# Layer 0's experts on one Trainium2 core: spreading routed vectors through DRAM in place of PE turns

## The chip, the core and the metric

The kernel runs on one core of a Trainium2 chip, as one launch. The metric is device time in microseconds (us), taken from the median of several runs; one further execution was recorded by the hardware profiler, and every profile line comes from that one. Engines are named as the profile names them: PE (matmuls, and turns by matmul with an identity), DVE, ACT and POOL (elementwise work), SP (which here only issues DMAs). ACT and POOL issue DMAs too.

## The reference, cut to what matters

Four layers follow each other; each adds a cross attention and a feed-forward part to `x` (4 sequences of 256 tokens, 256 wide, float32). The change lies in layer 0. Its feed-forward part routes every token to the 4 of 64 experts whose 16 projected values have the largest norm, sums the projections of the four, and sends the sum through all four's output matrices:

```python
x = x + _L0_xattn_ref(_layernorm(x), ctx, ...)      # 16 heads of width 16
x = x + _L0_ffn_ref(_layernorm(x), A, B, W, bias)

def _L0_ffn_ref(x, A, B, W, bias):                  # A: 64 x 16 x 256, B: 64 x 256 x 16
    vecs = jnp.einsum('arh,bsh->bsar', A, x)
    arrows = jnp.linalg.norm(vecs, axis=-1)
    _, idx = jax.lax.top_k(arrows, 4)
    routes = jax.nn.one_hot(idx, 64).sum(-2) / 4
    v = jnp.einsum('bsa,bsar->bsr', routes, vecs)
    delta = jnp.einsum('bsa,ajr,bsr->bsj', routes, B, v)
    return jnp.einsum('bsh,jh->bsj', x, W) + bias + delta
```

## The kernel before, in words

Tokens are worked in tiles of 128, two per sequence, so there are 8 tiles (n = 0 to 7; sequence n // 2). Everything named here is in `bounded_path`, in a block in which the code's order is the order on PE, ACT, DVE and POOL: nothing reorders instructions between the lines. SP takes its DMAs in code order as well.

**Opening** (lines 1057 to 1200, 1541 to 1600). DMAs bring the first sequence, the first context, the query, key and value weights and three rows of biases (`crow`, lines 1081 to 1086). The biases and weights are centred per head on DVE (`head_sums`, `centred`, lines 1173 to 1182). Three small matmuls spread the bias rows over 128 partitions (`spread_biases`, line 1188), with selecting rows `takes` that POOL makes (`rows_of_biases`, line 1120). `warm(n)` (line 1464) runs n matmuls of the identity that nothing reads.

**Layer 0's attention.** For each sequence b, eight half steps i (four head groups, two halves each) hold the scores of a head group on PE, their exponentials on ACT, and the values of the head group before. `between(b, i)` (line 1613) puts other work behind each half step: the next sequence's projections, the output of the sequence before, and in the last sequence the start of the experts. `quotient` (line 1428) divides a head group's values by its sums on DVE.

**Layer 0's experts.** `Arrows(n)` (line 1471) has a tile's steps:
- `vectors` (line 1479): four matmuls give 1024 projections per token; ACT copies and squares them into the two halves of the tile `two`.
- `routes` (line 1496): DVE sums the squares per expert, finds the four largest (lines 1502 to 1509), multiplies the projections by the 0 or 1/4 of their expert (line 1511) and sums over experts to the 16-vector `v` (line 1513). POOL then writes the product of route and `v`, 128 x 1024, over the squares (line 1514).
- `turned` (line 1516): PE turns this product in eight 128 x 128 pieces, ACT copies them to `uT`.
- `output` (line 1527): two pairs of matmuls (`ww`) and eight matmuls with `uT` (line 1535) accumulate the result; DVE adds the bias (line 1537), POOL adds it to `x` (line 1538).

The loop at line 1749 runs the tiles so that the routing of tile n + 2 comes before the turns and output of tile n. Between them it puts two kinds of other work: `layernorm_T` (line 939), which turns a sequence's normalized rows by four PE turns, and `next(fold)`: `folding` (line 1003) multiplies layer 1's raw attention weights into each other, 8 half folds, each with a group of matmuls whose results ACT and DVE copy. `load_raw` (line 987) brings these raw weights by SP's queue, four DMAs for each of four groups, with two groups' buffers.

Other parts of the kernel already turn rows without PE: `layernorm_aside` (line 969) turns 32 x 32 blocks on DVE and puts them in place by 16 DMAs on SP.

Of the kernel before, what the change touches and what calls it, by code (L numbers as in the profile page):

```python
# [9 lines left out]
F32 = mybir.dt.float32  # L10
# [826 lines left out]
def bounded_path(ctx: ExitStack, tc: tile.TileContext, t, out: bass.AP, over):  # L837
# [34 lines left out]
    def load_c(b):  # L872
        (nc.sync if b else nc.scalar).dma_start(c_sb[:, b], t["ctx"][b].rearrange("(k p) c -> p k c", p=P))
# [113 lines left out]
    def load_raw(L, i, after=None, tiles=None):  # L987

        wq, wk, wv, wo = (t[f"L{L}_{n}"] for n in ("wqT", "wkT", "wvT", "wo"))
        h0, g0 = 4 * i, 2 * i  # L990
        if tiles is None:
            tiles = [
                rawp.tile(shape, F32, tag=f"{n}_t", name=f"{n}_{L}_{i}")
                for n, shape in (("wq", [P, 4, D]), ("wk", [P, 2, DC]), ("wv", [P, 2, DC]), ("wo", [P, 4, D]))
            ]
        wq_t, wk_t, wv_t, wo_t = tiles
        for dst, src, a, z in ((wq_t, wq, h0, 4), (wk_t, wk, g0, 2), (wv_t, wv, g0, 2), (wo_t, wo, h0, 4)):
            dma = (nc.gpsimd if L == 2 else nc.sync).dma_start(dst, src[a * P : (a + z) * P, :].rearrange("(h e) d -> e h d", e=P))
            if after and L != 2:
                behind(dma, after)  # L1000
        raws[L, i] = wq_t, wk_t, wv_t, wo_t
# [53 lines left out]
    with tc.manual_schedule(engines={E.PE, E.Activation, E.DVE, E.Pool}):  # L1055
        c0 = ExitStack()
        l0 = c0.enter_context(tc.tile_pool(name="l0", bufs=1, side="right"))

        load_x(0)
        load_c(0)  # L1060
# [3 lines left out]
        wkv = l0.tile([P, 2, 2 * D], F32, tag="wkv", name="wkv")  # L1064
        nc.scalar.dma_start(wkv[:, 0, :], t["L0_wkv"])
# [5 lines left out]
        def by_head(w, x=HD0):  # L1071
            return w.rearrange("p n (h x) -> p n h x", x=x)


        rows1 = w0.tile([3, D + 3 * P], F32, tag="oT0", name="rows1")
        crow = rows1[:, :D].rearrange("n (o d) -> n o d", o=1)
        takes = rows1[:, D:].rearrange("n (i p) -> n i p", p=P)


        brow = l0.tile([1, 2, 2 * D], F32, tag="brow", name="brow")  # L1080
        nc.sync.dma_start(crow[0:1, 0, :], t["L0_bq"].partition_broadcast(1))
        for i, n in enumerate(("L0_bkv", "L0_bdca")):
            nc.sync.dma_start(
                crow[1 + i : 2 + i, 0, :].rearrange("o (h x) -> o h x", x=HD0),
                t[n].rearrange("(o h x) -> o h x", o=1, x=2 * HD0)[:, :, :HD0],
            )
# [16 lines left out]
        wb = load_fw("wb", [P, 8, D], lambda w: [(w, t["F0_bT"].rearrange("(k p) n -> p k n", p=P))], "wb", f0w)  # L1103
# [16 lines left out]
        def rows_of_biases():  # L1120
            nc.gpsimd.memset(takes, 1.0)
            for i, base, cm, p in (
                (0, 0, -1, 0), (1, -1, 1, 0), (1, 1, -1, 0), (2, RD - 1 - P, P, -1), (2, 2 * P - RD, -P, 1),
            ):
                nc.gpsimd.affine_select(
                    out=takes[:, i, :], in_=takes[:, i, :], compare_op=ALU.is_ge, fill=0.0, base=base,
                    pattern=[[p, P]], channel_multiplier=cm,
                )

        c_last = l0.tile([P, 2, 2, P], F32, tag="c_last", name="c_last")  # L1130
        nc.gpsimd.memset(c_last, 0.0)
# [56 lines left out]
        def spread_biases():  # L1188
            pb = bank("mm", [P, 2, D], "pbias0")
            for i in range(2):  # L1190
                nc.tensor.matmul(pb[:, i, :], lhsT=takes[:, i, :], rhs=crow[:, 0, :], start=True, stop=True)
            pl = bank("mm", [P, D], "pbias1")
            nc.tensor.matmul(pl, lhsT=takes[:, 2, :], rhs=crow[:, 0, :], start=True, stop=True)
            nc.scalar.copy(bqk[:, 0:2, :], pb)
            nc.scalar.copy(bqk[:, 2, :], pl)
# [111 lines left out]
        def columns_of_norms():  # L1307
# [5 lines left out]
            for o in range(2):  # L1313
                nc.vector.tensor_scalar(
                    cols[:, o, :], pairs[:, 0, :], halves0[:, o : o + 1], HD0 ** -0.5, ALU.mult, ALU.mult
                )
            nc.vector.tensor_copy(cols[:, 2:, :], pairs[:, 1:, :])
# [152 lines left out]

        class Arrows:
# [24 lines left out]
            def routes(self):  # L1496
# [11 lines left out]
                route = small.tile([P, NA], F32, tag="route", name=f"route{u}")  # L1508
                nc.vector.tensor_scalar(route, rest[:, :NA], 0.0, 1.0 / TOPA, ALU.is_lt, ALU.mult)
                route_b = route[:, :, None].to_broadcast([P, NA, RA])  # L1510
                nc.vector.tensor_tensor(ar, ar, route_b, ALU.mult)
                v = small.tile([P, RA], F32, tag="v", name=f"v{u}")
                nc.vector.tensor_reduce(v, ar.rearrange("p a r -> p r a"), AX.X, ALU.add)
                nc.gpsimd.tensor_tensor(sq, route_b, v[:, None, :].to_broadcast([P, NA, RA]), ALU.mult)

            def turned(self):
                self.uT = w0.tile([P, 8, P], F32, tag="qT0", name=f"uT{self.u}")
                for n in range(2):
                    pt = bank("t", [P, 4, P], f"puT{self.u}_{n}")
                    for k in range(4):  # L1520
                        a0 = 8 * (4 * n + k)
                        nc.tensor.transpose(
                            pt[:, k, :], self.two[:, 1, a0 : a0 + 8, :].rearrange("p a r -> p (a r)"), ident
                        )
                    nc.scalar.copy(self.uT[:, 4 * n : 4 * n + 4, :], pt)
# [15 lines left out]
        warm(9)  # L1541
        context_T(0)
        norm = Norm(0, "a0_0")
        rows_of_biases()
        last_context(0)
        mq = head_sums(by_head(wq0))
        xn = norm.tokens()
        warm(3)
        xnTs[0] = layernorm_T(xn, "a0_0")
        centred(by_head(wq0), by_head(wq0), mq)  # L1550
        centred(by_head(crow), by_head(crow), head_sums(by_head(crow), 3), 3)
# [6 lines left out]
        columns_of_norms()  # L1558
        warm(3)
        add_q = project_q(0)  # L1560
        spread_biases()
        add_q()
# [49 lines left out]

        def between(b, i):

            n = b + 1
            if n == 1:
# [76 lines left out]
            if b == B - 1:  # L1693
                if i in (0, 2, 6):
                    norms["f", i // 2] = Norm(min(i // 2, 2), f"f0_{min(i // 2, 2)}")
                if i in (1, 3, 7):
                    xns["f", i // 2] = norms["f", i // 2].tokens()
                if i in (3, 5):
                    k = (i - 3) // 2
                    xnTs["f", k] = layernorm_T(xns["f", k], f"f0_{k}")  # L1700
                if i == 4:
                    arrows[0] = Arrows(0)
                    arrows[0].vectors()
                if i == 5:
                    arrows[0].routes()
# [25 lines left out]
        arrows[1].routes()  # L1731
        arrows[0].turned()
        arrows[0].output()
        output0(B - 1)
# [14 lines left out]
        for n in range(B * NC):  # L1749
            if n + 2 < B * NC:  # L1750
                arrows[n + 2].routes()
            if n:
                arrows[n].turned()
            if n % NC == 0:
                if n + 3 < B * NC:
                    arrows[n + 3] = Arrows(n + 3)
                    arrows[n + 3].vectors()
                for _ in range((0, 0, 1, 1, 2, 2, 1, 1)[n]):
                    next(fold)
                if n == 6:  # L1760
                    xn1 = norm.tokens()
                if n:
                    arrows[n].output()
            else:
                k = n // NC + 2
                if k < B:
                    xnTs["f", k] = layernorm_T(xns["f", k + (k == 2)], f"f0_{k}")
                if n == 7:
                    first_xnT = layernorm_T(xn1, "a1_0")
                    next(fold)  # L1770
                arrows[n].output()
                for _ in range((0, 0, 1, 1, 2, 2, 1, 0)[n]):
                    next(fold)
                if n + 3 < B * NC:
                    arrows[n + 3] = Arrows(n + 3)
                    arrows[n + 3].vectors()
            if n == 5:
                norm = Norm(0, "a1_0")
            if n == 0:
                norm = Norm(3, "f0_3")  # L1780
            if n == 1:
                xns["f", 3] = norm.tokens()
            if 2 <= n < 2 + B:

                b = n - 2
                c2 = w0.tile([P, NK, DC], F32, tag="z0", name=f"c2_{b}")
                for k in range(NK):
                    nc.scalar.activation(
                        c2[:, k], c_sb[:, b, k], AF.Square, accum_out=csq[:, b * NK + k : b * NK + k + 1]
                    )  # L1790
# [1689 lines left out]
```

## Time and profile before

| what | value |
|---|---|
| median of 3 runs | 1381.64 us (1380.35 to 1382.58) |
| profiled execution | 1380.97 us, of it the span from first to last instruction 1379.2 us |
| PE busy in the span | 1369.2 us, 99% |
| DVE, POOL, ACT busy | 897.2, 699.4, 572.6 us |
| opening, to the first scores | 0 to 20.96 us |
| layer 0's attention | 20.96 to 137.39 us |
| layer 0's experts with layer 1's folds | 137.39 to 220.30 us, PE busy 82.91 us of it |
| DVE, ACT, POOL busy in the experts' stage | 58.06, 41.08, 26.09 us |
| the rest (layers 1 to 3) | 220.30 to 1379.2 us, PE busy 1150.95 us |

How to read its lines: a timeline line gives the start and the length in us, the engine, the line of the kernel, the operation, written tile<-read tiles, the shape and how many instructions are merged in it; in brackets the idle time of the engine ahead of it and what ended it. A matmul is recorded twice, in two halves, except a turn, which is one record; the end of a matmul reaches some 0.16 us into the next one. A window line gives the window, its length, the busy time of PE, weight loads, DVE, ACT and POOL with their counts, PE's granted clock as a share of full speed, the DMA engines' share and GB/s.

### The profile page before, as it was taken

Reading aid. Unit: us, or ns where it says so; the run is one execution under the profiler, and the core shown is the slowest. Engines: PE = TensorE matmul, PEld = TensorE weight load, DVE = VectorE, ACT = ScalarE, POOL = GpSimd, SP = SyncE. Lnnn points to the kernel's source line nnn. Section 1 sums busy time; section 2 is a strip of 40 time slices with the busy share of each in tenths; the row PEclk is TensorE's granted clock in tenths of the full one; section 3 lists DMA queues with packets and bytes.
Section 4 is the critical chain, followed back from the end, with each engine's and each line's share of the span. In section 5 each row is a group of like instructions: output and inputs, shape, how many; then the busy total and the mean of one; then the engine's idle time right before and its main releaser. Section 6 shows DMA issues by size and latency. Waiting matters only on the chain.

```text
span 1379.2 us, 20227 instructions
## 1 busy us (share of the span) xinstructions
PE 1369.2 (99%) x7221; PEld 903.1 (65%) x7221; DVE 897.2 (65%) x2052; ACT 572.6 (42%) x1134; POOL 699.4 (51%) x848
## 2 busy tenths in 40 slices
PE   9999999999999999999999999999999999999997
PEld 7665676566656667887565666666975665666666
DVE  6767863666666557655676756558656758566675
ACT  5766454433343332256434333333364334333331
POOL 5223333566565445352577655566325676444660
PEclk9999999999999999999999999999999999999999
DMA  5000220300000001361120000000432000000001
GB/s 171 15 3 2 77 78 17 89 19 8 16 5 19 0 13 43 83 218 48 47 54 15 17 0 16 0 1 16 124 119 69 7 12 4 1 8 1 0 1 34
DMA packets 77907, 50.79 MB, mean 37 GB/s; under 512 B 40628, under 2 KB 72645, under 8 KB 77799
## 3 DMA queue, kind: packets, MB, share of 16 engines
q1 hardware_dynamic: 72262, 36.13, 9.6%
q0 software_dynamic: 4176, 12.24, 3.1%
q8 instruction: 59, 0.97, 0.3%
q10 hardware_dynamic: 1360, 1.05, 0.2%
q14 instruction: 50, 0.40, 0.1%
HBM read 38.78 MB, written 6.95 MB: 33 GB/s over the span
## 4 chain that ended last, share of the span: by engine, by line
PE 97%; POOL 2%; DVE 1%; issue 0%; ACT 0%; POOLq 0%; DVEq 0%
PE ps L1948 23%; PE po L1956 23%; PE paq L1918 6%; PE pao L1918 5%; PE pbq L1918 4%; PE pbo L1918 4%; PE ps L1401 3%; PE po L1411 2%; PE pyf L1535 2%; PE paf L1485 2%; PE pgu L2496 2%; PE pm L1014 2%; PE psh L2317 2%; PE py L2042 2%; PE pn L1030 1%; PE pb L2901 1%
## 5 line engine op out<-in xcount | busy, mean ns | idle before, releaser
L1967 POOL TENSOR_TENSOR half<-pT 128x1024 f32<-128x1024 f32 x93 | 218.4, 2349 | 282.8 <-ACT pT L1951 228.0
L1948 PE MATMUL ps<-qT,cT 128*128 128x512 f32 x768 | 345.6, 593 | 0.0
L1956 PE MATMUL po<-pT,c_sb 128*128 128x512 f32 x768 | 345.3, 592 | 0.0
L1951 ACT ACTIVATE pT<-ps,mbias 128x512 f32<-128x512 f32 x384 | 263.8, 687 | 164.0 <-PE ps L1948 147.3
L1956 PEld LDWEIGHTS po<-pT,c_sb 128*128 128x128 f32 x768 | 145.8, 190 | 183.2 <-issue 183.2
L1948 PEld LDWEIGHTS ps<-qT,cT 128*128 128x128 f32 x768 | 138.9, 190 | 138.4 <-issue 136.1
L1960 ACT COPY oT<-po 128x512 f32<-128x512 f32 x96 | 56.2, 586 | 265.2 <-PE po L1956 265.2
L2003 POOL TENSOR_TENSOR oT<-oT,wide 128x512 f32<-128x512 f32 x84 | 106.8, 1291 | 0.0
L1928 DVE TENSOR_TENSOR qT<-qT,paq 128x128 f32<-128x128 f32 x90 | 25.2, 280 | 87.1 <-ACT qT L1927 87.1
L1405 ACT ACTIVATE pT<-ps 128x512 f32<-128x512 f32 x128 | 66.0, 602 | 21.6 <-PE ps L1401 21.4
L1975 DVE TENSOR_TENSOR half<-half 128x512 f32<-128x512 f32 x96 | 71.9, 749 | 2.7 <-POOL half L1965 2.5
L1977 DVE STREAM_TRANSPOSE turned<-half 128x512 f32<-128x512 f32 x96 | 68.3, 711 | 6.3
L1918 PE MATMUL paq<-xnT_a,m_sb 128*128 128x128 f32 x360 | 71.3, 280 | 0.0
L1928 DVE TENSOR_TENSOR w<-w,pao 128x128 f32<-128x128 f32 x21 | 6.0, 285 | 99.2 <-ACT w L1927 99.2
L1918 PE MATMUL paq<-xx,m_x 128*128 128x128 f32 x360 | 69.6, 275 | 0.0
L1918 PEld LDWEIGHTS paq<-xnT_a,m_sb 128*128 128x128 f32 x360 | 57.5, 192 | 18.2 <-issue 9.2
L1981 DVE TENSOR_REDUCE sums<-turned 128x16 f32<-128x512 f32 x96 | 65.9, 686 | 3.3
L1918 PE MATMUL pao<-n_x,ox 128*128 128x128 f32 x336 | 65.0, 275 | 0.0
L1927 ACT COPY qT<-paq 128x128 f32<-128x128 f32 x90 | 23.9, 265 | 94.2 <-PE paq L1918 93.2
L1931 DVE TENSOR_TENSOR qT<-qT,pbq 128x384 f32<-128x384 f32 x90 | 49.8, 554 | 9.4
L1918 PEld LDWEIGHTS paq<-xx,m_x 128*128 128x128 f32 x360 | 54.7, 192 | 0.0
L2002 DVE STREAM_TRANSPOSE wide<-rz 128x512 f32<-128x512 f32 x84 | 54.4, 686 | 0.0
(504 smaller groups left out, 2553.9 us busy)
## 6 DMA issues: line engine op xcount, KB each, us to landing
wq<-in_L_wqT SPq DMA_DIRECT2D x8, 512.0 KB
wo<-in_L_wo SPq DMA_DIRECT2D x8, 512.0 KB
yd<-yr SPq DMA_DIRECT2D x20, 128.0 KB
xnT_a<-y_a SPq DMA_DIRECT2D x144, 16.0 KB
xd<-xn_f SPq DMA_DIRECT2D x8, 256.0 KB
w<-in_F_w SPq DMA_DIRECT2D x4, 512.0 KB
wq<-in_L_wqT POOLq DMA_DIRECT2D x3, 512.0 KB
wo<-in_L_wo POOLq DMA_DIRECT2D x3, 512.0 KB
```

The lines of the kernel that those rows point to most:

```text
L1405: nc.scalar.activation(pT[kp][:, j], ps[j], AF.Exp)
L1918: nc.tensor.matmul(p[:, at, :], lhsT=lhsT, rhs=rhs, start=(k == 0 and at == 0), stop=(k == len(of) - 1 and i == which[-1]),)
L1948: nc.tensor.matmul(ps, lhsT=cT[:, b, k * P : (k + 1) * P], rhs=qT, start=True, stop=True)
L1951: nc.scalar.activation(pT[:, k, :], ps, AF.Exp, bias=mbias[:, b, k : k + 1])
L1956: nc.tensor.matmul(po, lhsT=c_sb[:, b, k, :], rhs=pT[:, k], start=(k == 0), stop=(k == NK - 1))
L1960: done["head"] = nc.scalar.copy(raw, po).ins
L1967: nc.gpsimd.tensor_tensor(half, pT[:, 0:2], pT[:, 2:4], ALU.add)
L1975: nc.vector.tensor_tensor(part, half[:, 0], half[:, 1], ALU.add)
L1977: nc.vector.transpose(turned.rearrange("p f i -> p (f i)"), part)
L1981: nc.vector.tensor_reduce(sums[b, hp // 4][:, hp % 4, :], turned, AX.X, ALU.add)
L2002: nc.vector.transpose(wide, rzs[b, hp // 4][:, hp % 4, :, None].to_broadcast([P, NB, 32]))
L2003: eng.tensor_tensor(outs[b, hp], outs[b, hp], wide.rearrange("p f i -> p (f i)"), ALU.mult)
```

## The change

1. **Turns.** Of a tile only two 128-wide pieces are turned on PE: the routes (written twice side by side, so that the turn has them on 128 partitions) and the 16-vector `v`. ACT copies both. The turned `v` (16 rows of 512 bytes) is written to a DRAM scratch by ACT's queue; SP then reads it back with two DMAs, each of which gives 64 partitions the same 4 KB (8 rows of `v`). POOL multiplies what has landed by the turned routes (`spread`), and the result takes the place of `uT`. The rows of `wb` are loaded in an order that fits.
2. **Order.** The loop over tiles is written out by hand, with `spread` of a tile just ahead of its `output`, and with other distances between `routes`, `turned` and `output`.
3. **Raw weights.** Layer 1's raw weights are loaded by POOL's queue: groups 0 and 1 behind the spread of tile 1, group 2 behind that of tile 4, group 3 behind that of tile 5.
4. **Expert rows.** For sequences 0 to 2 the normalized rows of the experts are turned by `layernorm_aside`, from the third sequence of layer 0's attention on; sequence 3 keeps its PE turns. Tile 0's vectors, routing, turns and spread move to earlier half steps of the last sequence.
5. **Opening.** The bias rows are loaded first, by ACT's queue, ahead of the context and of the key and value weights. `takes` is copied from the identity by DVE. The bias rows are centred and spread ahead of the queries; 11 warm matmuls at the start take the place of 9 and two times 3.

```diff
-            dma = (nc.gpsimd if L == 2 else nc.sync).dma_start(dst, src[...])
+            dma = (nc.gpsimd if L < 3 else nc.sync).dma_start(dst, src[...])
...
-                route = small.tile([P, NA], F32, tag="route", name=f"route{u}")
-                nc.vector.tensor_scalar(route, rest[:, :NA], 0.0, 1.0 / TOPA, ALU.is_lt, ALU.mult)
...
-                nc.gpsimd.tensor_tensor(sq, route_b, v[:, None, :].to_broadcast([P, NA, RA]), ALU.mult)
+                self.route = sq.rearrange("p a r -> p (a r)")[:, : 2 * NA].rearrange("p (h a) -> p h a", h=2)
+                nc.vector.tensor_scalar(
+                    self.route, rest[:, None, :NA].to_broadcast([P, 2, NA]), 0.0, 1.0 / TOPA, ALU.is_lt, ALU.mult
+                )
...
             def turned(self):
-                for n in range(2):
-                    pt = bank("t", [P, 4, P], f"puT{self.u}_{n}")
-                    for k in range(4):
-                        nc.tensor.transpose(pt[:, k, :], self.two[:, 1, a0 : a0 + 8, :]..., ident)
-                    nc.scalar.copy(self.uT[:, 4 * n : 4 * n + 4, :], pt)
+                pt = bank("t", [P, 2, P], f"prT{self.u}")
+                nc.tensor.transpose(pt[:RA, 1, :], self.v, ident)
+                nc.tensor.transpose(pt[:, 0, :], self.route.rearrange("p h a -> p (h a)"), ident)
+                nc.scalar.copy(vT, pt[:RA, 1, :])
+                put = turned_v[self.b * NC + self.c]
+                nc.scalar.dma_start(put, vT)
+                nc.scalar.copy(self.routeT, pt[:, 0, :])
+                for h in range(2):
+                    nc.sync.dma_start(
+                        two[64 * h : 64 * h + 64, 1],
+                        put[8 * h : 8 * h + 8].rearrange("(o k) s -> o (k s)", o=1).to_broadcast([64, 8 * P]),
+                    )
+
+            def spread(self):
+                nc.gpsimd.tensor_tensor(self.uT, self.uT, self.routeT[:, None, :].to_broadcast([P, 8, P]), ALU.mult)
```

The experts' stage after the last values, as it is written out now (`vectors(1)`, `routes(1)`, `vectors(2)`, `routes(2)`, `output` of tile 0, `turned` of tile 1 and the attention's last output stand ahead of it; `output(n, ...)` is spread, raw loads, output; `Norm` and `tokens` are DVE work of a layer norm):

```python
vectors(3);  norm = Norm(3, "f0_3")
arrows[2].turned();  vectors(4);  arrows[3].routes();  vectors(5)
output(1, 0, 1);  arrows[3].turned();  arrows[4].routes();  xn3 = norm.tokens()
output(2);  context_squares(0);  arrows[4].turned()
next(fold);  xnTs["f", 3] = layernorm_T(xn3, "f0_3");  next(fold)
arrows[5].routes();  vectors(6);  arrows[5].turned()
output(3);  context_squares(1);  arrows[6].routes();  vectors(7)
next(fold);  next(fold);  arrows[6].turned()
output(4, 2);  context_squares(2);  arrows[7].routes();  arrows[7].turned()
output(5, 3);  context_squares(3);  norm = Norm(0, "a1_0")
next(fold);  next(fold);  xn1 = norm.tokens()
output(6);  next(fold);  first_xnT = layernorm_T(xn1, "a1_0");  next(fold)
output(7)
```

## The prediction

> **What bounds the kernel now.** I read the page's engine rows, then the chain of work that ended last, then the timeline of layer 0's experts by engine. The first three lines are from the page, the rest from the timelines of PE, DVE and POOL and from the stage windows.
>
> ```profile
> span 1379.2 us, 20227 instructions
> PE   9999999999999999999999999999999999999997
> PE 97%; POOL 2%; DVE 1%; issue 0%; ACT 0%; POOLq 0%; DVEq 0%
> ```
> ```profile
> 1.53 4.21 PE L1468 MATMUL pwarm<-ident 128*128 128x128 f32 x18 [1.53 <-POOL ident masks.py:199]
> 5.53 1.06 PE L911 MATMUL pcT<-ident,c_sb 128*128 128x128 f32 x4
> 6.38 1.30 PE L1468 MATMUL pwarm<-ident 128*128 128x128 f32 x6
> 7.52 0.60 PE L945 MATMUL pxn_a<-ident,xn_a 128*128 128x128 f32 x4
> ...
> 154.90 1.04 PE L1522 MATMUL puTf<-ident,twof 128*128 128x128 f32 x8
> 155.77 0.60 PE L945 MATMUL pxn_f<-ident,xn_f 128*128 128x128 f32 x4
> 156.21 1.03 PE L1531 MATMUL pyf<-ww,xnT_f 128*128 128x256 f32 x4
> 157.07 3.62 PE L1535 MATMUL pyf<-wb,uTf 128*128 128x256 f32 x16
> ```
> ```profile
> 197.55 0.42 DVE L1537 TENSOR_TENSOR ysf<-pyf,bias 128x256 f32<-128x256 f32 x1 [3.70 <-PE pyf L1535]
> 197.91 1.21 DVE L1502 TENSOR_REDUCE nrf<-twof 128x64 f32<-128x1024 f32 x1
> ...
> 201.44 1.90 DVE L1513 TENSOR_REDUCE vf<-twof 128x16 f32<-128x1024 f32 x1
> ```
> ```profile
> 198.05 0.73 POOL L1538 TENSOR_TENSOR x_sb<-x_sb,ysf 128x256 f32<-128x256 f32 x1 [4.52 <-DVE nrf L1501]
> 203.48 1.93 POOL L1514 TENSOR_TENSOR twof<-routef,vf 128x1024 f32<-128x1024 f32 x1 [4.70 <-DVE vf L1513]
> ```
> ```profile
> 1375.00:1376.00 1.00, 0.00 (x0) 0.00 (x0) 0.00 (x0) 0.00 (x0) 0.00 (x0) 1.00 0.05 16
> 1376.00:1377.00 1.00, 0.00 (x0) 0.00 (x0) 0.00 (x0) 0.00 (x0) 0.00 (x0) 0.55 0.08 25
> ```
>
> PE holds the path nearly everywhere; the experts' stage (137.39 to 220.30, 82.9 us) has no PE gap. So PE work removed there is gained in full, and every wait put before PE is lost in full. Rows overlap by a matmul's tail; I price a step by the next row's start. The DVE rows show a chain that PE hides today: bias sum, then a tile's routing, to 203.34. The last rows give PE's clock (the column after the counts): PE's last matmul ends at 1372.0, and the grant is halved from 1376.1.
>
> **What goes.** A tile's eight turns cost 0.87 (154.90 to 155.77), 0.109 each; two stay, 0.22. Over 8 tiles 5.2 us. Three of four turns of normalized rows (L945, 0.44 each, 155.77 to 156.21) go to DVE and DMAs: 1.3 us. Together **-6.5**.
>
> **What waits come in.** Of tile n: Vn its vectors (PE 3.43: 160.52 to 163.96), Rn routing (DVE 5.43: 197.91 to 203.34), Tn its two turns (0.22), On its output (0.86, then 3.45 behind the spread product; 3.62 to its last end). F is half a fold (179.96 to 181.72, 1.75), X a turn of rows (0.44). From V1 the new PE order is V1 V2 O0 T1, attention output (1.7), V3 T2 V4 V5 O1 T3 O2 T4 F X F V6 T5 O3 V7 F F T6 O4 T7 O5 F F O6 F X F O7: 76.6 us without waits. DVE and POOL take their work in code order, which makes four waits:
>
> - **T7 behind O4.** DVE has O4's bias sum ahead of R7, and PE has nothing between O4 and T7. O4's tail 0.16, wake-up 0.11, sum 0.36 to the next row, R7 5.43, wake-up 0.1: **6.2**.
> - **T5 behind V6.** R5 stands behind the copy of the second F's result (L1033: 181.92, 0.05 after its matmul's end, 0.2 after PE is free; 0.61 to the next row). 0.2 + 0.61 + 5.43 + 0.1 less V6's 3.43: **2.9**.
> - **O2 behind O1.** POOL adds O1 to x before it multiplies tile 2's spread. From O1's tail: 0.16 + 0.11, 0.5 to the add (197.55 to 198.05), 0.69, product 1.93, 0.1 = 3.5, less T3 and O2's first part (1.08): **2.4**. The eight raw loads before that add issue on POOL in 6.2 (0.78 each, the median of layer 2's on POOL), from 22.3 after V1's start to 28.5, as O1's sum ends (28.5): hidden, but with nothing to spare. The product has another operand form; L1967's full 128x1024 product takes 2.35, so this wait is 2.4 to 2.8.
> - **O6 behind O5.** Sum, norm statistics (206.78 to 208.15), power (208.23, 0.70), product: 4.8 less F F and 0.86: **0.4**.
>
> The clock that these use, in us from V1's start. DVE: tile rows of sequence 2 (tokens 1.0, two block turns 0.8) and the last quotient (139.93 to 141.57 with its first turn 0.70: 2.3) to 4.2; R1, once ACT has copied V1, to 10.1; R2 to 15.4; three sums (0.4 each, one held 0.5 by POOL's add) to 17.1; POOL adds the last of them by 18.0; norm of sequence 3 to 19.6, POOL's power to 20.4, its product for tile 1 to 22.3. DVE's R3 runs 19.6 to 24.9, O1 ends on PE at 27.9, its sum at 28.5, R4 at 33.9. O2 starts its long part at 31.4, T4 is due at 34.9.
>
> Sum **+11.9**. T1 to T4 and T6 are hidden: R1 ends at 10.1 and T1 is due at 11.2, R2 at 15.4 against 16.5, R4 at 33.9 against 34.9, R6 6.1 after O3 against V7 and F F, 6.9. Those margins are about 1 us.
>
> **DRAM trip.** No row shows it whole. A store's row: the experts' store at 630.4 lets its gather start at 632.9, 2.5. Landings end the other way with the bias rows, issued at 2.84 and awaited until 8.71: 5.9. Store, two issues and a broadcast load cost 6 to 13. I take 6 to 7, nearest to the store, the only DRAM scratch. The shortest cover is tile 1's, T1's end (11.4) to a product begun by 22.6: 11.2. So 0, at worst +1.6. Rows of tile 2 go as 16 DMAs (0.64 each: twelve in 7.70 us) from 1.9 to 12.2, past which T1's spread queues on SP; V4 wants them at 16.8. Hidden. The first raw weights are issued on POOL at 22.3 and wanted at 34.9; 2.6 MB at the opening's 211 GB/s take 12.4: hidden, at worst +2.
>
> **PE's clock.** Nothing here shows an idle PE in mid-kernel. From the rows: the grant fell 4.1 us after PE stopped, and the wait at T7 is 6.2, so it can fall there; the opening's pitch (18 rows in 4.0 us, against 0.109 per turn from 7.52) stays at half speed until 7.4, 5.8 after PE's first matmul. 5.8 us at half speed lose 2.9; if the fall misses, 0. I take **+2.5**, by the idle row.
>
> [...]
>
> **Opening.** Before, centred bias rows arrive late (DVE waits for them at 8.71), the spread matmuls stand behind the queries, ACT ends their copy at 12.46 and DVE adds the queries at 12.50. Now the rows go first; queries follow three spread matmuls (1.3) and end near 11.4: -1.1. Against it, PE's first 11 matmuls end at 6.2 and PE then idles to 7.4. [...] I take **-0.4**, between the two, as the moment of the rise is loose.
>
> **Layer 0's third sequence.** Tile 0's rows put a token pass (0.72) and two block turns (0.41 each) ahead of head sums at 95.70. ACT took their result 0.9 late anyway, so 0.6 passes on; the scaled heads end near 102.5, PE wants them at 102.38: **+0.2**. V0, R0 and T0 lie earlier in the fourth sequence; PE work is equal, DVE had gaps (4.27 before 129.02).
>
> **Sum.** -6.5 + 11.9 + 2.5 + 0.2 - 0.4 = +7.7 on the profiled execution (span 1379.2, 1380.97 with what lies around it): 1388.7. The runs' median, 1381.64, lies 0.67 above that, so 1389.3; I say **1389**.
>
> **Rivals.**
> 1. *Waits without the clock.* The halving misses or PE resumes before it. For it: nothing shows a fall in mid-kernel. +5.2: 1386.9.
> 2. *The DRAM trip or raw loads decide.* Both use the same DMA engines from 22 on. For it, the 5.9 landing; against it, covers above 11. +7.7 and 1.6 to 3.6: 1391 to 1393.
> 3. *Faster: routing stays hidden.* In the kernel before, each routing runs two tiles ahead and PE never waits. If DVE reached R5 and R7 before the copies and sums named, 9.1 and the clock's 2.5 vanish: -3.9, 1377.7. It decides once all waits sum to less than 6.7. Against it: the built order on DVE has them behind.
> 4. *Nothing to measure.* Favourable ends throughout (opening -1.1, no clock loss, products and routing slightly shorter): +2, 1384.
>
> **How the numbers follow.** Forecast 0.60 (1387.5 to 1391), first rival 0.20, second 0.09, third 0.05, fourth 0.06. Low end: first rival with the opening at -1.1 and some more, 1385. High end: the product at 2.35 (+0.8 over two waits), opening +0.6, the late trip: 1393. A run here tells from no change what is over 0.2%, 2.8 us. Slower 0.89, same 0.06, faster 0.05.
>
> **What would show it.** PE rows of the stage: turns 0.22; idle before the first turn of tile 7 about 6 <-DVE, of tile 5 about 3 <-DVE, before the long part of O2 about 2.4 <-POOL; stage length near 91 with the clock loss, 88.5 without. The granted clock below 1 after T7. First scores near 20.5 instead of 20.96. Wrong: PE waiting for DMAs in those rows, routing well under 5 us, or no PE gap at T7.

## The result, and the profile after

The changed kernel takes 1397.3 us (median of 4 runs, 1396.95 to 1398.93) against 1381.21 of the kernel before: ratio 1.0116, interval 1.0102 to 1.0129. It is slower by 16.1 us. The forecast was slower by 7.7, in a range that ended at 1393. Sign and main mechanism held, the size did not. Runs of one kernel differ by up to 4.6 us: in one series the kernel before took 1380.2 to 1380.9 us at a granted clock of 0.999, and 1383.3 to 1383.6 at 0.996.

The page of the changed kernel, span, PE's row of tenths and the chain that ended last:

```profile
span 1395.8 us, 20244 instructions
...
PE   8999988999999999999999999999999999999998
...
PE 90%; DVE 4%; POOL 3%; DMA 1%; issue 1%; ACTq 0%; ACT 0%; DVEq 0%; POOLq 0%; SPq 0%
```

PE held 97% of the chain and now holds 90%; DVE has grown from 1% to 4%, POOL from 2% to 3%, and a DMA has come in. The tenths under 9 show where: the first slice, and the sixth and seventh (174 to 244 us), the experts' stage; the last is the kernel's end, as before. Setting the starts of the same PE instructions of both traces side by side gives the account:

| stretch | before | after | difference |
|---|---|---|---|
| opening, to the first scores | 20.96 | 25.78 | +4.8 |
| first scores to V1 (layer 0's attention) | 116.43 | 115.77 | -0.7 |
| V1 to layer 1's first queries (experts' stage) | 82.91 | 94.01 | +11.1 |
| from there to behind layer 1's list matmuls (`plist`) | 351.75 | 354.91 | +3.2 |
| from there to the last matmul | 799.72 | 799.60 | -0.1 |
| last matmul to the end | 7.43 | 5.77 | -1.7 |

The opening on PE (timeline; start, length, tiles, in brackets the wait ahead and what ended it):

```profile
1.53 5.06 PE L1464 MATMUL pwarm<-ident 128*128 128x128 f32 x22 [1.53 <-POOL ident masks.py:199]
6.54 0.96 PE L945 MATMUL pxn_a<-ident,xn_a 128*128 128x128 f32 x4
9.91 0.66 PE L911 MATMUL pcT<-ident,c_sb 128*128 128x128 f32 x4 [2.40 <-DMA c_sb<-in_ctx]
10.49 2.83 PE L1186 MATMUL pbias<-rows 3*128 3x256 f32 x6
13.25 3.78 PE L1204 MATMUL pq<-wq,xnT_a 128*128 128x256 f32 x8
```

Before, the context's turns ran at 5.53 with no wait. Now PE waits 2.4 for the context's load, and the queries behind take 3.78 instead of 1.99: PE has lost half its clock (granted 0.50 from 10.63 to 17.46). The stage on PE, cut to its waits and what follows them:

```profile
173.41 5.41 PE L1544 MATMUL pyf<-wb,twof 128*128 128x256 f32 x16 [2.54 <-POOL twof L1532]
...
189.12 0.28 PE L1519 MATMUL prTf<-ident,vf 128*16 128x128 f32 x1 [2.71 <-DVE vf L1512]
...
212.76 0.37 PE L1519 MATMUL prTf<-ident,vf 128*16 128x128 f32 x1 [7.09 <-DVE vf L1512]
212.93 0.42 PE L1520 MATMUL prTf<-ident,twof 128*128 128x128 f32 x1
213.14 1.92 PE L1540 MATMUL pyf<-ww,xnT_f 128*128 128x256 f32 x4
214.85 3.91 PE L1544 MATMUL pyf<-wb,twof 128*128 128x256 f32 x16
...
223.74 3.72 PE L1544 MATMUL pyf<-wb,twof 128*128 128x256 f32 x16 [0.61 <-POOL twof L1532]
```

These are the four waits of the forecast, at O2, T5, T7 and O6, with the releasers it named. After two of them half the clock is gone (granted 0.50 from 174.47 to 177.88 and from 208.60 to 215.43): 5.41 instead of 3.62 for O2's long part, 1.92 instead of 1.03 for the first part of T7's neighbour O5.

The clock, by stretches. In this trace every change of the grant lies on one grid of 3.413 us (from 10.63 to 590.90 they are 1 to 108 such steps apart), so I cut the trace along it. Columns: window, length, busy time of PE, weight loads, DVE, ACT and POOL with counts, PE's granted clock, the DMA engines' share, GB/s.

```profile
7.22:10.63 3.41, 1.01 (x8) 0.60 (x7) 1.42 (x3) 0.61 (x2) 0.00 (x0) 1.00 0.95 305
10.63:14.04 3.41, 3.41 (x8) 2.30 (x9) 2.62 (x7) 1.52 (x3) 2.63 (x12) 0.50 1.01 311
...
171.06:174.47 3.41, 1.06 (x5) 0.96 (x6) 3.14 (x7) 1.05 (x8) 2.29 (x1) 1.00 0.71 238
174.47:177.88 3.41, 3.41 (x10) 2.71 (x9) 2.81 (x4) 0.00 (x0) 0.00 (x0) 0.50 0.52 145
184.71:188.12 3.41, 1.70 (x4) 0.39 (x3) 3.10 (x8) 2.15 (x4) 0.00 (x0) 1.00 0.01 2
188.12:191.53 3.41, 2.42 (x13) 2.16 (x14) 0.94 (x1) 1.61 (x10) 0.00 (x0) 1.00 0.03 7
...
580.66:584.07 3.41, 3.38 (x30) 3.15 (x28) 3.41 (x17) 0.00 (x0) 0.00 (x0) 1.00 0.00 0
584.07:587.48 3.41, 3.41 (x13) 2.96 (x13) 1.41 (x10) 0.00 (x0) 0.93 (x1) 0.50 0.00 0
```

Read them in pairs: a window in which PE was busy for 1.01 or 1.06 is followed by one at half clock, one with 1.70 is not. So a wait of 2.5 at O2 cost a half clock, and one of 2.7 at T5, which the grid cut in two, did not. The last pair is the +3.2 of layer 1: PE is busy for 3.38, yet the grant falls. All but 0.1 of that window is list matmuls, 40 columns wide. Before, the grid lay otherwise (counted in such steps back from the fall at 1376.1, its windows began at 563.73 and 567.15) and split the same matmuls 1.7 and 2.4, with the grant at 1.00 in both.

### The profile page after: what moved, and what is told of

Same layout as the page of the kernel before. It is cut to its first block, busy times and chain, and to the rows that moved or that the text cites. A ratio compares the mean times of both kernels' runs of the same rounds, so it can differ in the third digit from the quotient of the medians.

```text
span 1395.8 us, 20244 instructions
## 1 busy us (share of the span) xinstructions
PE 1371.9 (98%) x7153; PEld 901.9 (65%) x7153; DVE 902.7 (65%) x2062; ACT 567.2 (41%) x1131; POOL 712.4 (51%) x858
## 4 chain that ended last, share of the span: by engine, by line
PE 90%; DVE 4%; POOL 3%; DMA 1%; issue 1%; ACTq 0%; ACT 0%; DVEq 0%; POOLq 0%; SPq 0%
PE ps L1982 23%; PE po L1990 23%; PE paq L1952 6%; PE pao L1952 5%; PE pbq L1952 4%; PE pbo L1952 4%; PE ps L1397 2%; PE pgu L2530 2%; PE po L1407 2%; PE psh L2351 2%; PE py L2076 1%; PE pyf L1544 1%; PE pm L1014 1%; PE pn L1030 1%; PE pb L2935 1%; PE pyb L2961 1%
```

## The experiments

The theory was: the opening (+4.8), the waits and the clock behind them make up the loss; all come from where instructions stand, and none from the way by DRAM. The main rivals: that way or the raw weights set the pace underneath, and what runs long behind the waits is itself waiting for something else. Differences below are medians against runs of the kernel before on the same chip in the same series (the changed kernel: +16.1); positions are from each run's trace.

### The opening

**x1_opening_before**: the changed kernel with the old opening, context first on ACT's queue and bias rows on SP's behind `wq0`.

```diff
+        load_c(0)
-        nc.scalar.dma_start(crow[...], ...)
+        nc.sync.dma_start(crow[...], ...)
...
-        warm(11); rows_of_biases(); ...; spread_biases(a, z)(); ...; project_q(0)()
+        warm(9); context_T(0); ...; warm(3); ...; warm(3); project_q(0); spread_biases()
```

> The changed kernel with the opening of the kernel before: context first on ACT's queue, bias rows on SP's, selecting rows made by POOL, bias matmuls behind the queries, warm matmuls 9, 3 and 3. Theory (the changed opening is a term of its own: PE waits for the context, then runs 6.8 us at half clock): first scores at 20.96 as before instead of 25.78, so 4.8 off 1397.3: 1392.5, give or take 3.1 for whether the clock falls in layer 1 at the list matmuls. Rival (the opening's loss is made good later, since the first exponentials wait for other things): within 1 us of 1397.3.

Measured: +9.3 (1391.45; ratio 1.0065, 1.0045 to 1.0085); first scores at 20.75. The opening's term is real and is not made good later: from first scores to V1 it is 115.79 here and 115.77 with the late opening.

**x2_context_first**: one move.

```diff
+        load_c(0)
         nc.scalar.dma_start(crow[0:1, 0, :], ...)
...
-        load_c(0)
         nc.scalar.dma_start(wkv[:, 0, :], t["L0_wkv"])
```

> The changed kernel with one thing moved: the first context's load stands first on ACT's queue, ahead of the three bias rows. Theory (the late context is the cause): the context is there by 6, PE has no wait of 2.4 before its turns; the bias rows land 0.6 later, so PE may wait 1 for them; first scores near 21.5, 1393. Rival (the bias matmuls, which fill only 3 of 128 rows, hold the clock down wherever they stand): the clock still halves after them, first scores at 23 or later, 1395.

Measured: +11.8 (1393.94); first scores at 24.27. The wait for the context went, but two short ones came (0.71 ahead of the first turns, 0.62 ahead of the bias matmuls, whose rows now land later), and the clock fell at 9.61 for two windows all the same (0.89 granted over the first 30 us, against 1.00 in x1). Theory half right: the late context was not the whole cause. The rival that the three-row bias matmuls hold the clock down was still open.

**x3_warm_opening**: the wait is filled, not shortened.

```diff
+        warm(24)
         context_T(0)
         last_context(0)
```

> The changed kernel with 24 more warm matmuls on PE ahead of the context's turns, which fill the wait of 2.4 us without shortening it. Theory (most of the opening's loss is the clock, not the wait): the clock stays full from 7.2 on, bias and query matmuls take 1.3 and 1.9 instead of 2.8 and 3.8, first scores near 22.6, 1394.1. Rival one (the wait itself is the loss): first scores at 25.8, 1397.3. Rival two (the bias matmuls bring the clock down by themselves): the clock falls at 14.0 instead of 10.6, about 1 us gained, 1396.

I had sized the filler wrongly: a warm matmul shows as two records of 0.11, so 24 take 5.4 and not 2.6. Measured: +14.9; first scores at 25.17. The trace tells the cases apart still:

```profile
12.68 0.60 PE L911 MATMUL pcT<-ident,c_sb 128*128 128x128 f32 x4
13.21 1.56 PE L1186 MATMUL pbias<-rows 3*128 3x256 f32 x6
14.70 1.99 PE L1204 MATMUL pq<-wq,xnT_a 128*128 128x256 f32 x8
```

Bias matmuls and queries are back at 1.5 and 1.8 from start to start, and the grant stays full through the opening from 7.15 on (1.00 over the first 30 us). From the start of the bias matmuls to the keys it is 3.32 against 6.33, and the first keys take 1.30 instead of 1.61: some 3.3 of the 4.8 us are clock, the rest the wait.

**x5_first_and_warm**: x2, with two more warm matmuls at the start and three in its second gap.

```diff
+        load_c(0)
...
-        warm(11)
+        warm(13)
...
+        warm(3)
         for a, z in ((0, 2), (2, 3)):
             spread_biases(a, z)()
```

> The changed kernel with the context's load first on ACT's queue, two more warm matmuls at the start (13) and three ahead of the bias matmuls, which fill the two waits of 0.7 and 0.6 us that the run with the context first still had. Theory (the opening's loss is the late context and the gaps by which the clock falls): the clock rises near 7 and stays, bias matmuls 1.5, queries 1.9, first scores near 21.2 instead of 25.78, 4.6 off 1397.3: 1392.7. Rival (bias matmuls with 3 rows bring the clock down by themselves): half clock again for two windows, scores at 23.5 or later, 1395.

Measured: +11.5 (1392.31); first scores at 20.92, grant full through the opening from 4.65 on:

```profile
7.13 0.75 PE L945 MATMUL pxn_a<-ident,xn_a 128*128 128x128 f32 x4 [0.96 <-DVE xn_a L933]
...
8.92 1.56 PE L1186 MATMUL pbias<-rows 3*128 3x256 f32 x6
10.41 1.99 PE L1204 MATMUL pq<-wq,xnT_a 128*128 128x256 f32 x8
```

The rival falls: the same three-row matmuls run at full clock here. Without the late context and without the half clock the opening's loss is gone, and the new order of biases and queries in itself gains nothing (20.92 against 20.96). What kept the clock is not settled. The second gap was filled, but the first was not (0.96 against 0.71 in x2), since the clock rose earlier, at 4.65 instead of 6.20, and the warm matmuls ended sooner; the grid lay otherwise as well.

**x11_opening_alone**: the kernel before with the new opening and nothing else (the diff of x1 the other way round).

> The kernel before with the changed opening alone (bias rows first on ACT's queue, bias matmuls ahead of the queries, 11 warm matmuls at the start and none behind). Theory: PE waits some 2.5 for the context and runs two windows at half clock; first scores near 25.8 instead of 20.96, 4.8 more than before's 1381: 1386, up to 1389 if the shift lets the clock fall at layer 1's list matmuls. Rival (the opening costs only together with the other edits): 1381.

Measured: +9.8 (1390.50; ratio 1.0069, 1.0052 to 1.0086), above what I expected. First scores at 28.19, the other stretches as before (116.43, 82.91), but for one window of half clock at the list matmuls (1.4 more than before from there to the last matmul). Its opening:

```profile
11.10 1.12 PE L911 MATMUL pcT<-ident,c_sb 128*128 128x128 f32 x4 [3.64 <-DMA c_sb<-in_ctx]
12.15 2.92 PE L1185 MATMUL pbias<-rows 3*128 3x256 f32 x6
```

The context, issued at 2.71 as in the changed kernel, landed at 11.1 here and at 9.9 there, with the DMA engines' share at 0.99 and 0.95 in the window ahead of the landing, and the half clock lasted three windows instead of two. So the opening costs 4.8 to 7.2 in these two traces. The other runs with this opening, x10, x8, x6 and x4, have their first scores at 26.04, 27.19, 27.89 and 28.99: how late the context comes varies from profile to profile, and the whole times of these runs hold that too.

### The stage's waits

**x6_order**: PE's order kept, DVE's and POOL's changed.

```diff
         xn3 = norm.tokens()
+        arrows[5].routes()
         output(2)
...
-        output(3); context_squares(1); arrows[6].routes(); vectors(7)
+        arrows[6].routes(); output(3); context_squares(1); vectors(7); arrows[7].routes()
...
         def output(n, *raw):
-            arrows[n].spread()
             for i in raw:
                 load_raw(1, i)
+            if n < 7:
+                arrows[n + 1].spread()
             arrows[n].output()
```

(For tile 1: spread 1, raw group 0, spread 2, raw group 1, output.)

> The changed kernel with another order on DVE and POOL in the experts' stage, PE's order kept: the routings of tiles 5, 6 and 7 stand ahead of the bias sums of tiles 2, 3 and of the folds' copies, and each tile's spread product stands ahead of the addition to x of the tile before. Theory (the stage's waits come from that order, and the half clocks from the waits): the waits of 2.5, 2.7, 7.1 and 0.6 go and the half clocks with them (1.7 and 1.7): stage near 77.5 instead of 94.0, 1380.8. Rival (the way by DRAM, or the raw weights by POOL's queue, set the pace underneath): waits for DMAs show in their place, stage 85 or more, 1388.

Measured: +1.2 (1382.02; ratio 1.0004, 0.9994 to 1.0014). The stage takes 78.89 instead of 94.01, 1.4 above the forecast because a wait of 1.5 at T4 was left; no wait for a DMA is in it. The rival falls. That the time is above 1380.8 is the opening once more: the context came late by 3.6, first scores at 27.89.

**x7_order_opening**: x6 with the old opening.

> The run before with the opening of the kernel before as well. Theory: both terms go, 16.6 and 4.8: 1376, 0.4% faster than the kernel before, as the removed turns say (-6.5) less what attention gains or loses. Rival (DMAs underneath): 1383 or more.

Measured: -6.7 (1374.14; ratio 0.9951, 0.9934 to 0.9967). Stage 78.89 again, first scores at 20.45, granted clock 1.00 in the stage and 0.999 over the run. With order and opening both put right the change is a gain.

**x9_route_four**: x7, and one routing more ahead.

```diff
+        arrows[4].routes()
         arrows[1].spread()
         load_raw(1, 0)
...
-        arrows[4].routes()
         xn3 = norm.tokens()
```

> The run with both the new order and the opening of before, and one more routing ahead: tile 4's stands ahead of the bias sum of tile 1 on DVE. There the last wait of the stage was left, 1.5 at the turns of tile 4. Theory (routings behind sums are what PE waits for): the wait goes, stage near 77.4, 1374.1 - 1.5 = 1372.7. Rival (the sum of tile 1, now 2 later, holds up the additions and the norm behind it): a wait of 1 to 2 elsewhere, 1374.

Measured: -7.3 (1373.37; ratio 0.9946, 0.9929 to 0.9963). T4's wait went, but one of 1.35 came at T7: half of the theory, half of the rival. Stage 78.34.

### The clock in the stage

**x4_warm_stage**: the two longest waits filled with warm matmuls.

```diff
+        warm(20)
         output(2)
...
         arrows[7].routes()
+        warm(56)
         arrows[7].turned()
```

> The changed kernel with 20 warm matmuls (2.1 us) ahead of the output of tile 2 and 56 (6.0 us) ahead of the turns of tile 7: PE's two longest waits of the experts' stage are filled, not shortened. Theory (each wait costs a half clock after it besides itself: 1.7 at tile 2, 1.7 at tile 7): the granted clock stays full through the stage, stage 90.6 instead of 94.0, 1393.9. Rival (what runs slowly behind the waits waits for something else): stage unchanged, 1397.

Measured: +19.9 (1402.04), a miss by the same slip as in x3: the fillers take twice what I meant, and lengthen the stage to 99.4. Only one thing can be read: behind both fillers the clock is full (O2's long part 3.62, O5's first part 1.03).

**x8_warm_stage_fit**: the same with 10 and 27.

> The run that filled the stage's waits with too many warm matmuls (they take 0.22 each, two records of 0.11), with 10 and 27 instead of 20 and 56: 2.2 us ahead of the output of tile 2 and 6.0 ahead of the turns of tile 7. Theory (each wait costs a half clock besides itself): clock full after both, stage 90.6 instead of 94.0, or 92.3 if it falls at the wait for tile 5 instead; 1394 to 1396. Rival (what is slow behind the waits waits for something else): stage 94, 1397.

Measured: +14.8 (1395.65); stage 92.82. The falls behind O2 and T7 are gone (T7 to the next fold 4.5 instead of 5.8), and with the shifted grid the clock now falls at T5's wait (O3's long part 5.30 instead of 3.62). So the long rows behind the waits are the clock, each fall worth 1.3 to 1.8, and the same wait of 2.71 at T5 brought one here and none in the changed kernel, where the grid lay otherwise.

### The wait at T7, and raw weights

The forecast had 6.2 for this wait, the trace 7.09. The routing of tile 7 on DVE, and what POOL did then:

```profile
208.11 1.28 DVE L1507 TENSOR_SCALAR twof<-restf 128x128 f32<-128x128 f32 x1
...
210.76 1.86 DVE L1512 TENSOR_REDUCE vf<-twof 128x16 f32<-128x1024 f32 x1
```
```profile
206.97 2.34 POOL L1532 TENSOR_TENSOR twof<-twof 128x1024 f32<-128x1024 f32 x1
```

DVE's write of the routes takes 1.28 here and ends at 209.39, as POOL's product ends (209.31). In the routing of tile 5, with POOL idle, it takes 0.23.

**x10_product_five**: tile 5's product moved ahead.

```diff
         def output(n, *raw):
-            arrows[n].spread()
+            if n != 5:
+                arrows[n].spread()
+            if n == 4:
+                arrows[5].spread()
```

> The changed kernel with one edit: tile 5's spread product on POOL stands right behind tile 4's, so that it no longer runs beside the routing of tile 7. Theory (DVE's write of the routes, 1.28 instead of 0.23 in that routing, is held until POOL's product ends): the write takes 0.23, the wait before the turns of tile 7 falls from 7.1 to 6.0, the time by 1.0. Rival (the write is slow for another reason, such as its operands): 1.28 and 7.1 again.

Measured, one run: 1395.64. The write takes 0.37, with POOL issuing DMAs beside it and no product, and the wait is 6.17, near to what the theory had:

```profile
208.40 0.37 DVE L1507 TENSOR_SCALAR twof<-restf 128x128 f32<-128x128 f32 x1
```

So the write was long beside the product, and ended 0.08 behind it (209.39 and 209.31), and short without it. By what means the product holds it up, no run shows.

**x13_raw_earlier** and **x14_issues_behind**, on x9, whose write of tile 7's routes took 3.36 and whose T7 waited 1.35:

```diff
# x13
-        output(3)
+        output(3, 2)
...
-        output(4, 2)
+        output(4)
# x14, in output()
+            if n < 7:
+                arrows[n + 1].spread()
             for i in raw:
                 load_raw(1, i)
-            if n < 7:
-                arrows[n + 1].spread()
```

> The run with tile 4's routing ahead, with raw weights' group 2 issued on POOL ahead of tile 4's spread product instead of ahead of tile 5's. Theory (the write of tile 7's routes, 3.36 there, was held by POOL's four issues and the product behind them): the product runs some 2.9 earlier, the write takes 0.4 to 1.5, the wait of 1.3 at the turns of tile 7 falls to 0 to 0.3, 1373.4 - 1.2 = 1372.2. Rival (DVE itself or the folds' copies make tile 7 late): wait 1.3 again, 1373.4.

> The run with tile 4's routing ahead, with the raw weights' issues of tiles 4 and 5 behind the next tile's spread product instead of ahead of it, so that the write of tile 7's routes falls among DMA issues with no product behind them. Theory one (only the product holds the write): 0.4, till the product ends. Theory two (POOL's issues hold it as well, back to back): 3, till the last issue ends, and the wait at the turns of tile 7 stays 1 or more.

Measured: x13 -8.1 (1373.20; ratio 0.9936, 0.9920 to 0.9953). The wait at T7 is gone, and the stage has none left:

```profile
136.78:213.66 76.88, 76.88 (x331) 54.43 (x328) 58.55 (x103) 35.91 (x116) 40.50 (x39) 1.00 0.45 122
```

The time itself hardly moved against x9; in this profile the list matmuls cost 1.7 of half clock that x9 did not pay (granted 0.998 over the run against 0.999). x14, one run: 1373.72; the write takes 0.32 and ends with the product, with DMA issues directly behind. Issues alone did not hold it (0.37 in x10). But in x9 the write lasted from amid the issues, 0.9 ahead of the product behind them, until that product's end (190.64 and 190.55), and in x13 tile 6's write took 2.98 in the same way (182.84 and 182.75). Why it did not end in between is open. In x14 PE waits 1.2 for the raw weights instead, which now come too late.

**x12_raw_by_SP**: x9 with layer 1's raw weights on SP.

```diff
-            dma = (nc.gpsimd if L < 3 else nc.sync).dma_start(dst, ...)
+            dma = (nc.gpsimd if L == 2 else nc.sync).dma_start(dst, ...)
```

> The run with tile 4's routing ahead, with layer 1's raw weights back on SP's queue. Theory (where the raw weights are issued decides nothing, as POOL has slack): within 1 us of that run, 1372.7. Rival (on SP the loads wait for their buffers and hold the spread vectors of the next tiles behind them, or on POOL they hold the additions): 2 or more apart.

Measured: -5.6 (1375.13; ratio 0.9959, 0.9944 to 0.9973), 1.8 above x9, the ratios' intervals overlapping. The trace has the rival's mechanism: PE waits 1.54 at O2. SP's queue, then POOL:

```profile
153.57 0.38 SPq L998 DMA_DIRECT2D wq<-in_L_wqT  x1
154.00 1.52 SPq L998 DMA_DIRECT2D wk<-in_L_wkT  x1
...
157.74 1.09 SPq L1535 DMA_DIRECT2D twof<-turned_v  x2
```
```profile
164.63 2.83 POOL L1541 TENSOR_TENSOR twof<-twof 128x1024 f32<-128x1024 f32 x1 [6.18 <-DMA twof<-turned_v]
```

Tile 2's vectors are issued behind four raw loads and land at 164.6, some 6 after their issue. With the raw weights on POOL's queue, in x9, PE has no wait at O2, but the write of tile 7's routes takes 3.36 and PE waits 1.35 at T7; in x12 that wait is gone. The two waits nearly cancel (stage 78.65 against 78.34).

## Why the prediction was wrong

- **What goes, -6.5: right.** With no wait left the stage takes 76.88 against 82.91, -6.0, and the attention stretch loses 0.65: -6.7. The forecast for these two, with the third sequence's +0.2, was -6.3.
- **The four waits, +11.9: right in place and releaser, a little small.** 2.54, 2.71, 7.09 and 0.61, and 0.22 at T6, make 13.2. T7's extra 0.9 is the held write, which also ate the "about 1 us" of margin at T6. x6 shows that they come from DVE's and POOL's order: with it changed all five are gone, and 1.48 at T4 is new.
- **The clock, +2.5: mechanism right, size too small.** I let one wait pay, the longest. In the stage two did (3.1 together). The 4.1 us I read off the kernel's end was no measure for a wait here: 2.54 at O2, which left PE busy for 1.06 of one window, brought a fall, while the wait at O2 in x2, which left 1.54 in the window that held most of it, brought none. And the shift of everything behind moved layer 1's list matmuls into one window, +3.2, which I had not looked for.
- **The opening, -0.4: wrong, and the largest miss.** "Now the rows go first" priced what comes earlier, not what comes later: the first context, moved behind three issues on ACT's queue, landed at 9.9. Its issue moved by only 1.9 (from 0.81 to 2.71); SP also issues the second sequence and its context ahead of it now, at 1.72 and 2.23 instead of 4.75 and 5.21. What share these have, no run shows; x2 shows that context first on ACT's queue is enough to end the wait for it. PE's 11 warm matmuls were over at 6.6, and with the two sets of three gone nothing filled the gap; so the wait and two windows of half clock came together, +4.8. The -0.4 lay between a gain of 1.1 and +0.6 for a late rise of the clock, which the range used too; no run shows that second term, and the runs showed a fall after the rise instead.
- **The way by DRAM and the raw weights, 0: right.** No wait of the changed kernel's stage ends with a DMA; store and broadcast take 2.1 and 3.8 from issue to landing (medians). Which queue brings the raw weights made no difference clear of the noise (x12 against x9); with the order of the changed kernel it was not tried.
- **The end, not foreseen: -1.7.** From last matmul to the end every kernel with the new experts takes 5.7 to 5.9, before and x11 7.4. Nothing in the traces tells why; it was not tried.
- **The rivals.** The third, routing stays hidden, was given 1377.7 if DVE's order allowed it. x7, x9 and x13 are that case made true, at 1373.2 to 1374.1. The first (no fall of the clock) is out by x8, the second (DRAM) by x6, the fourth (nothing to measure, 1384) by the result.

Sum of the misses in the profiled execution: opening 5.2, waits 1.3, clock of the stage 0.6, list matmuls 3.2, end -1.7: 8.6 of the 8.9 by which its span passed the forecast of +7.7.

## What to carry to other kernels

A change that removes PE work but adds a longer chain on other engines is worth only what the order of those engines lets through: here nearly the same PE work is +16.1 or -8.1 us against the kernel before, by where some routings, products and loads stand. When loads are reordered at the start, price the one that now comes last, and look at what PE does while it waits. Count a PE wait twice, once for itself and once for the half clock that it may bring (at O2 2.54 and 1.8), and remember that a shift in time moves all that lies behind it against the clock's windows (at the list matmuls +3.2).

## What the runs showed of the hardware

- **The clock's windows.** In the changed kernel's trace the grant changes at 10.63, 17.46, 174.47, 177.88, 208.60, 215.43, 584.07 and 590.90, all on one grid of 3.413 us. In the experts' stage a wait of PE was followed by a fall where the window had PE busy for 0.49 (T7) and 1.06 (O2) in the changed kernel, 1.14 (T5) in x1 and 1.33 (T5) in x5, and by none where it had 1.54 (O2) in x2 and 1.70 (T5) in the changed kernel. The windows of x5 and x2, each with the one behind it:

```profile
182.14:185.55 3.41, 1.33 (x8) 1.20 (x9) 1.99 (x2) 1.01 (x5) 0.00 (x0) 1.00 0.03 7
185.55:188.97 3.42, 3.42 (x10) 2.70 (x9) 0.00 (x0) 1.17 (x8) 0.00 (x0) 0.50 0.03 7
```
```profile
170.04:173.45 3.41, 1.54 (x7) 1.39 (x8) 3.13 (x7) 0.57 (x4) 1.81 (x1) 1.00 0.60 197
173.45:176.87 3.42, 3.42 (x22) 2.99 (x21) 2.71 (x4) 0.55 (x3) 0.63 (x1) 1.00 0.59 149
```

In the changed kernel the grant was back after one window behind O2's fall (174.47 to 177.88, PE busy for 3.41) and after two behind T7's (208.60 to 215.43, PE busy for 0 and 2.67). In the openings, where three-row matmuls and gaps lie in between, half clock lasted two windows (the changed kernel, x2) or three (x11).
- **A fall with PE shown busy.** In the changed kernel list matmuls of 40 columns filled 3.3 of one window (580.66 to 584.07, PE busy for 3.38), and the grant was 0.50 in the next two; that cost 3.2. Before, the same matmuls lay 1.7 and 2.4 in two windows, with PE busy for 3.42 and 3.38, and the grant stayed at 1.00. A window with PE busy for 2.08, all turns and three-row matmuls but for a few warm ones, also ended in a fall (x2's opening, 6.20 to 9.61). What sets these windows apart, no run shows.
- **A held write.** DVE's 128x128 write of the routes took 0.23 beside an idle POOL (tile 5, the changed kernel), 1.24 to 2.06 beside POOL's product (the changed kernel, x7, x13, x14), and 2.98 (x13) and 3.36 (x9) where DMA issues stood ahead of that product; it ended within 0.1 of the product's end each time. Where it met only the product's last part (x14) or issues with no product behind them (x10), it took 0.32 and 0.37.
